# Order of the first FFN group, shared weight buffers, and paced normalizations in a macaron block

## The chip, the cores and the metric

The kernel runs on one core of one Trainium2 chip. The metric is the device time of one execution in microseconds (us); lower is better. The times are medians over runs, and one further execution of each kernel is recorded by the hardware profiler. The engines are named as in the profile: PE is TensorE (matrix products and transposes), DVE VectorE, ACT ScalarE, POOL GpSimd, and SP the engine whose queue issues the loads and stores.

## The reference

The block takes x of 2048 tokens by 512 features, all in float32, and runs an FFN at half weight, a causal attention with 16 heads of 32 features, and the same FFN with the same weights again:

```
x = x + 0.5 * ffn(layernorm(x))
x = x + attention(layernorm(x))
x = x + 0.5 * ffn(layernorm(x))

def ffn(xt):
    gate = einsum('th,nh->tn', xt, Wg)      # 512 -> 4096
    up   = einsum('th,nh->tn', xt, Wu)      # 512 -> 4096
    inter = gelu(gate) * up                 # tanh form
    return einsum('tn,hn->th', inter, Wd)   # 4096 -> 512
```

Wg, Wu and Wd come as 4-bit codes (two in each int32) with one scale for every 32 values, and have to be dequantized.

## The kernel before

**Order.** The program order of an engine's instructions is its order on the chip: the kernel writes out by hand which instruction follows which, and an instruction at the head of an engine's queue that waits holds up what stands behind it. Tiles come from pools; a new tile in a buffer waits until the readers of the old one are done.

**Tokens.** x stays in on-chip memory as 16 tiles of 128 tokens (`xs`), taken as four blocks of 512 (NB) and two pairs of blocks: pair 0 is the early tokens (blocks 0 and 1), pair 1 the late ones (2 and 3).

**Normalization** (`norm_steps`, L79). For a block: moments of each tile on DVE (L88, L89), a square root on ACT for all four tiles (L95) and a reciprocal on DVE (L96). Then, for each tile, the normalized tile xn, on DVE (L107) or with `on_act` on ACT (L105, with a bias from L98), four transposes on PE (L115) and a copy from PSUM on ACT (L116). The steps come as a list: two of statistics (`stats`, two tiles each), then normalize 0, normalize 1, transpose 0, and so on in alternation.

**FFN** (`ffn`, L132). The 4096 hidden features are handled in 8 groups of 512, a group in two row halves: `rows` and `second`, objects of `Rows` (L201) that hold seven weight combinations each for gate and up. In place of eight block products a Strassen-Winograd scheme uses seven, so the weights and the tokens need sums of blocks: the weights' on POOL (L223 to L226), the tokens' by `token_sums` (L238, four operations for a pair of blocks).

A `slot` (L269) is one row half with one pair of blocks: 7 gate products, then 7 up products, each of two 128x512 matmuls in float32 (L264), which the trace records as four matmuls. A product ends in a PSUM bank (a pool of seven) and is evicted on DVE or ACT with additions (L299 to L323); Gelu is on ACT (L282), gate times up on DVE (L286). Behind each product a slot calls `pump(rate)`, which takes `rate` steps from the list `background`, and pops one token sum and one down piece if it has any. The order of products is 1, 2, 6, 7, 5, 4, 3; the first two need no token sum, and the third needs the third sum.

A group is four slots: rows with pair 0, rows with pair 1, second with pair 0, second with pair 1. The 14 down pieces of a token pair (`down_pieces`, L331, matmuls L359) are put into a later slot, those of the last pair behind the last slot, where up to two steps of the next stage's normalization follow each piece from the third on.

**Weights.** In the first FFN they are dequantized on DVE (ten operations per 512 columns of codes, L184 to L192 and L180), and kept in DRAM (L199). The second FFN loads them from there (L210, L457). An FFN has its own two buffers for row halves; the attention has its own buffers for wqk (two pairs of heads at a time), wv, wo and the biases, which it loads at its start, and the second FFN issues its first load when it starts.

**Start of an FFN** (L424 to L455). In the first FFN: normalization of block 0, dequantization of gate, normalization of block 1, the sums of pair 0 on DVE, dequantization of up; then the first slot. Into `background` go the normalizations of blocks 2 and 3, the sums of pair 1 on POOL, and `second`'s dequantization; the first slot runs with rate 4. In the second FFN, blocks 0 and 1 come normalized from the attention's end.

**Attention** (L482). It normalizes blocks 2 and 3 itself, runs over 8 pairs of heads (p) with the projections of later pairs between, divides by the softmax's sums at the end (L687), and closes with the output projection (L572). The projection of heads is `project_qk` (L523), which loads its weights when it is called.

Of the kernel before, what the change touches and what calls it, by code (L numbers as in the profile page):

```python
# [9 lines left out]
F32 = mybir.dt.float32  # L10
F16 = mybir.dt.float16
BF16 = mybir.dt.bfloat16
# [6 lines left out]
P = 128  # L19
S = 2048  # L20
# [14 lines left out]
def macaron_kernel(ctx: ExitStack, tc: tile.TileContext, x, packed, scales, wqk, bqk, wv, bv, wo, bo, out):  # L35
# [16 lines left out]

    xpair = [res.tile([P, 2, D], F32, tag=f"x{t}", name=f"x{t}") for t in range(NT // 2)]
# [11 lines left out]
    nc.gpsimd.memset(eps, EPS)  # L65
    ones_b = const.tile([P, P], BF16, tag="ones_b", name="ones_b")
# [12 lines left out]
    def norm_steps(phase, tb, t_out, temp, on_act=False):  # L79

        nm = f"{phase}_{tb}"
        mv = small.tile([P, 4, 2], F32, tag="mv", name=f"mv_{nm}")
        rstd = small.tile([P, 4], F32, tag="rstd", name=f"rstd_{nm}")
        nbias = small.tile([P, 4], F32, tag="nbias", name=f"nbias_{nm}")

        def moments(i):
            st = small.tile([P, 6], F32, tag="st", name=f"st_{nm}_{i}")
            nc.vector.bn_stats(out=st, in_=xs[4 * tb + i])  # L88
            nc.vector.bn_aggr(out=mv[:, i, :], in_=st)  # L89

        def stats(i):
            moments(i)
            moments(i + 1)
            if i == 2:
                nc.scalar.activation(rstd, mv[:, :, 1], AF.Sqrt, bias=eps)  # L95
                nc.vector.reciprocal(rstd, rstd)  # L96
                if on_act:
                    nc.vector.scalar_tensor_tensor(nbias, mv[:, :, 0], -1.0, rstd, ALU.mult, ALU.mult)  # L98

        xn = [None] * 4  # L100

        def normalize(i):
            xn[i] = temp(f"xn_{nm}_{i}")
            if on_act:
                nc.scalar.activation(xn[i], xs[4 * tb + i], AF.Identity, bias=nbias[:, i : i + 1], scale=rstd[:, i : i + 1])  # L105
            else:
                nc.vector.tensor_scalar(  # L107
                    xn[i], xs[4 * tb + i], mv[:, i, 0:1], rstd[:, i : i + 1], ALU.subtract, ALU.mult
                )

        def transpose(i):
            xnv = xn[i].rearrange("t (jc p b) -> t jc b p", jc=2, b=2)
            pt = ps_one.tile([P, 4, P], F32, tag="one", name=f"pt_{nm}_{i}")
            for k in range(4):
                nc.tensor.transpose(pt[:, k, :], xnv[:, k // 2, k % 2, :], ident)  # L115
            nc.scalar.copy(t_out[:, :, i * P : (i + 1) * P], pt)  # L116

        steps = [lambda i=i: stats(i) for i in (0, 2)]
        for i in range(5):
            if i < 4:  # L120
                steps.append(lambda i=i: normalize(i))
            if i > 0:
                steps.append(lambda i=i: transpose(i - 1))
        return steps

    def x_transposed(phase, tb):
        return res.tile([P, 4, 512], F32, tag=f"xT{tb}", name=f"xT_{phase}_{tb}")
# [4 lines left out]
    def ffn(phase, finish, behind, ready=()):  # L132
# [8 lines left out]
        with tc.tile_pool(name=f"w{phase}", bufs=1) as wp, tc.tile_pool(name=f"dq{phase}", bufs=1) as dq, tc.tile_pool(  # L141
# [59 lines left out]
            class Rows:  # L201
# [3 lines left out]
                def __init__(self, g, h):  # L205
                    self.w = wp.tile([P, 2, 7, 2, P], F32, tag="w", name=f"w_{phase}_{g}_{h}", bufs=2)
                    self.g, self.h = g, h
                    self.codes = [None, None]
                    if phase == 2:
                        nc.sync.dma_start(out=self.w, in_=kept[g, h])  # L210
# [18 lines left out]
                def keep(self):  # L229
                    keep((self.g, self.h), self.w)  # L230
# [38 lines left out]
            def slot(g, rows, tp, sums, fill, rate):  # L269

                b = token_factors(tp)
# [16 lines left out]
                for m, done in ((0, gelu), (1, gated)):  # L288
# [7 lines left out]
                    for i in ORDER:  # L296
# [27 lines left out]
                        pump(rate)  # L324
                        if sums:
                            sums.pop(0)()
# [97 lines left out]
            rows = Rows(0, 0)  # L424
# [6 lines left out]
            for tb in range(NB):  # L431
                xT[tb] = ready[tb] if tb < len(ready) else x_transposed(f"f{phase}", tb)
            norms = [norm_steps(f"f{phase}", tb, xT[tb], normed) if tb >= len(ready) else [] for tb in range(NB)]
            run(norms[0])
            if phase == 1:
                run(rows.steps(0))
            run(norms[1] + token_sums(0, nc.vector))
            if phase == 1:
                run(rows.steps(1))
            background += norms[2] + norms[3] + token_sums(1, nc.gpsimd)  # L440
            fill = ([], [])
            for g in range(NG):
                second = Rows(g, 1)
                if phase == 1:
                    for m in range(2):
                        second.load(m)
                    for m in range(2):
                        background += second.steps(m)
                    rows.keep()
                first = [slot(g, rows, 0, *fill, 2 if g > 0 else 4)]  # L450
                pump(1 << 30)
# [6 lines left out]
                first.append(slot(g, rows, 1, [], [], 1))  # L458
                last = [slot(g, second, 0, [], [], 1)]
# [8 lines left out]
                if phase == 1:  # L468
                    keep(g, wd)
                last.append(slot(g, second, 1, *fill, 2))  # L470
# [3 lines left out]
            steps = behind(normed)  # L474
            for i, piece in enumerate(fill[1]):
                piece()
                if i > 1:
                    run(steps[:2])
                    del steps[:2]
            run(steps)  # L480

    def attention(xT, xT_f):  # L482
        with tc.tile_pool(name="aw", bufs=1) as aw, tc.tile_pool(name="qk", bufs=1) as qkp, tc.tile_pool(
            name="pp", bufs=3
        ) as pp, tc.tile_pool(name="an", bufs=2) as an:
            wqk_sb = aw.tile([P, 2, 4, P], F32, tag="wqk", name="wqk_0")
            nc.sync.dma_start(out=wqk_sb, in_=wqk[0])
            wv_sb = aw.tile([P, 4, D], F32, tag="wv", name="wv_sb")
            bv_sb = aw.tile([P, D], F32, tag="bv", name="bv_sb")
            bqk_sb = aw.tile([P, 2, NQ], F32, tag="bqk", name="bqk_sb")  # L490
            bo_sb = aw.tile([P, D], F32, tag="bo", name="bo_sb")
            wo_sb = aw.tile([P, 4, D], F32, tag="wo", name="wo_sb")
            nc.sync.dma_start(out=bqk_sb, in_=bqk)
            nc.sync.dma_start(out=wv_sb, in_=wv)
            nc.sync.dma_start(out=bv_sb, in_=bv.partition_broadcast(P))
# [6 lines left out]

            mrow = qkp.tile([P, S], BF16, tag="mrow", name="mrow")
# [19 lines left out]
            def project_qk(u):  # L523

                w = wqk_sb
                if u > 0:
                    w = aw.tile([P, 2, 4, P], F32, tag="wqk", name=f"wqk_{u}")
                    nc.sync.dma_start(out=w, in_=wqk[u])

# [268 lines left out]
            }  # L798
            for p in range(NPAIR):
                fills = plan[p]() if p in plan else [[] for _ in range(NB)]  # L800
# [46 lines left out]
    xT_a = []  # L847

    def norms_behind(temp):
        steps = []  # L850
        for tb in range(2):
            xT_a.append(x_transposed("a", tb))
            steps += norm_steps("a", tb, xT_a[tb], temp)
        return steps

    ffn(1, lambda t: None, norms_behind)
    xT_f = []
    attention(xT_a, xT_f)
    ffn(2, lambda t: nc.sync.dma_start(out=out[t * P : (t + 1) * P, :], in_=xs[t]), lambda temp: [], xT_f)
# [64 lines left out]
```

## Time and profile before

| | us |
|---|---|
| runs | 3348.92, 3349.23, 3352.65 |
| median | 3349.23 |
| profiled execution: its time | 3353.61 |
| its span in the trace | 3351.8 |

The mean clock granted to PE over the span is 0.991 of full speed. The page cuts the span into 40 equal slices of 83.8 us. A digit is the busy share in tenths, 9 is 90% or more:

```
PE   5999999999999989999999999899999999999998
DVE  7887777877777555676766784444445455444545
ACT  2111111111111121455543455421111111111111
POOL 2456464644646441322212222122132222313223
PEclk8999999999999999999999999899999999999999
DMA  3111111111111110000000000100110101011101
```

The first FFN takes the first 14 slices, the attention the next 12, the second FFN the rest. PE is busy throughout but in the first slice, in slice 15 (the first FFN's end and the attention's start) and in slice 26 (the attention's end and the second FFN's start). DVE is busier in the first FFN than in the second, which has no dequantization.

Lines of the timeline read: start in us, duration, engine, name of the result where it is one group, line of the kernel, operation, out<-in, shape, count. A bracket gives the idle time of the engine ahead of the line and what ended it.

### The profile page before, as it was taken

The numbers are of one execution on the slowest core, as the hardware profiler recorded it, in microseconds if no ns is written. First come the engines' busy times: TensorE is split into PE (matmuls) and PEld (weight loads), VectorE is DVE, ScalarE is ACT, GpSimd is POOL, SyncE is SP. The second block draws the span as 40 slices with busy tenths as digits, with TensorE's granted clock in tenths as the row PEclk, the third lists the DMA queues.
The fourth block names the chain that finished last, engine by engine and source line by source line (L and its number), as shares of the span: only waits on it lengthen the run. The fifth ranks groups of instructions, "written<-read, shape, count | busy, mean of one in ns | idle before, by whom it ended". The sixth has DMA issues, their size and how long they took to land.

```text
span 3351.8 us, 34007 instructions
## 1 busy us (share of the span) xinstructions
PE 3276.4 (98%) x12640; PEld 1734.2 (52%) x12640; DVE 2128.5 (64%) x3242; ACT 848.4 (25%) x1766; POOL 1157.9 (35%) x1337
## 2 busy tenths in 40 slices
PE   5999999999999989999999999899999999999998
PEld 3556565655656565333344333346565565656556
DVE  7887777877777555676766784444445455444545
ACT  2111111111111121455543455421111111111111
POOL 2456464644646441322212222122132222313223
PEclk8999999999999999999999999899999999999999
DMA  3111111111111110000000000100110101011101
GB/s 104 73 66 66 66 42 68 63 47 68 65 63 48 44 38 7 6 13 6 7 12 4 6 7 7 69 22 22 44 44 28 60 23 44 22 44 44 44 22 51
DMA packets 37941, 132.73 MB, mean 40 GB/s; under 512 B 3984, under 2 KB 20368, under 8 KB 31376
## 3 DMA queue, kind: packets, MB, share of 16 engines
q1 hardware_dynamic: 37776, 130.57, 10.7%
q8 instruction: 99, 1.62, 0.2%
q14 instruction: 66, 0.54, 0.1%
HBM read 78.12 MB, written 48.23 MB: 38 GB/s over the span
## 4 chain that ended last, share of the span: by engine, by line
PE 96%; DVE 3%; ACT 1%; issue 0%; POOL 0%; DMA 0%; SPq 0%; POOLq 0%; ACTq 0%; DVEq 0%
PE po L359 23%; PE pu L264 23%; PE pg L264 23%; PE av L667 8%; PE pm L610 6%; PE pqk L533 4%; PE ps L702 3%; PE ps L711 2%; PE pp L572 2%; PE pv L550 2%; PE pt_f L115 1%; DVE st_f L88 0%; PE pt_a L115 0%; DVE parts L625 0%; PE row L646 0%
## 5 line engine op out<-in xcount | busy, mean ns | idle before, releaser
L264 PE MATMUL pg<-xT_f,w 128*128 128x512 f32 x1024 | 481.6, 599 | 9.4 <-DVE st_f L88 8.0
L359 PE MATMUL po<-wd,inter 128*128 128x256 f32 x2048 | 484.4, 381 | 0.0
L264 PE MATMUL pu<-xT_f,w 128*128 128x512 f32 x1024 | 475.9, 593 | 0.0
L359 PEld LDWEIGHTS po<-wd,inter 128*128 128x128 f32 x2048 | 391.0, 191 | 154.8 <-issue 105.0
L370 POOL TENSOR_TENSOR x<-x,d 128x512 f32<-128x512 f32 x256 | 339.8, 1338 | 352.4 <-DVE d L367 175.7
L316 POOL TENSOR_TENSOR u<-u,u 128x512 f32<-128x512 f32 x128 | 163.2, 1275 | 853.6 <-ACT u L313 845.3
L625 DVE TENSOR_REDUCE parts<-pm 128x1 f32<-128x512 f32 (+3 forms) x640 | 367.3, 604 | 92.9 <-PE pm L610 81.6
L359 PE MATMUL po<-wd,s 128*128 128x256 f32 x1536 | 363.9, 381 | 0.0
L264 PE MATMUL pg<-xsum,w 128*128 128x512 f32 x768 | 356.9, 594 | 0.0
L264 PE MATMUL pu<-xsum,w 128*128 128x512 f32 x768 | 355.4, 593 | 0.0
L359 PEld LDWEIGHTS po<-wd,s 128*128 128x128 f32 x1536 | 293.3, 191 | 116.1 <-issue 79.4
L610 PE MATMUL pm<-kT,qT 32*128 32x512 f32 (+3 forms) x1280 | 338.1, 574 | 0.5 <-DVE parts L625 0.4
L734 ACT ACTIVATE pt<-ps 128x512 f32<-128x512 f32 (+3 forms) x576 | 271.8, 531 | 149.6 <-PE ps L711 148.9
L667 PE MATMUL av<-pt,vaug 128*64 128x512 f32 (+3 forms) x1280 | 304.2, 554 | 0.8 <-ACT both L676 0.6
L264 PEld LDWEIGHTS pg<-xT_f,w 128*128 128x128 f32 x1024 | 196.3, 192 | 205.7 <-issue 188.6
L264 PEld LDWEIGHTS pu<-xT_f,w 128*128 128x128 f32 x1024 | 194.9, 190 | 193.4 <-issue 182.6
L711 PE MATMUL ps<-qT,kT 32*128 32x512 f32 (+3 forms) x1280 | 292.9, 531 | 0.0
L264 PEld LDWEIGHTS pu<-xsum,w 128*128 128x128 f32 x768 | 146.2, 190 | 145.0 <-issue 138.1
L264 PEld LDWEIGHTS pg<-xsum,w 128*128 128x128 f32 x768 | 146.3, 191 | 142.7 <-issue 134.0
L367 DVE SCALAR_TENSOR_TENSOR x<-po,x 128x512 f32<-128x512 f32 x192 | 131.6, 686 | 118.5 <-ACT d L374 85.8
L687 POOL TENSOR_TENSOR attnT<-both,den 32x128 f32<-32x128 f32 x256 | 115.2, 450 | 242.9 <-DVE den L684 174.6
L367 DVE SCALAR_TENSOR_TENSOR d<-po,d 128x512 f32<-128x512 f32 x192 | 131.7, 686 | 84.3 <-PE po L359 82.9
(126 smaller groups left out, 3644.5 us busy)
## 6 DMA issues: line engine op xcount, KB each, us to landing
kept<-wd SPq DMA_DIRECT2D x8, 1792.0 KB
wd<-kept SPq DMA_DIRECT2D x8, 1792.0 KB
x<-in_x SPq DMA_DIRECT2D x16, 256.0 KB
pk<-in_gate_codes SPq DMA_DIRECT2D x16, 256.0 KB
sc<-in_gate_scales SPq DMA_DIRECT2D x32, 128.0 KB
pk<-in_up_codes SPq DMA_DIRECT2D x16, 256.0 KB
sc<-in_up_scales SPq DMA_DIRECT2D x32, 128.0 KB
pk<-in_down_codes SPq DMA_DIRECT2D x16, 256.0 KB
```

The source lines that it names most:

```text
L264: nc.tensor.matmul(ps, lhsT=a[:, j, :], rhs=b[:, j, :], start=(j == 0), stop=(j == 1))
L316: nc.gpsimd.tensor_tensor(u4, u4, u2, ALU.add)
L359: nc.tensor.matmul(ps[:, j, :], lhsT=a[i][:, k, bass.ts(2 * q + j, P)], rhs=b[i][:, k, :], start=(k == 0), stop=(k == 1),)
L367: stt(dst, ps, 0.5, other, ALU.mult, ALU.add)
L370: nc.gpsimd.tensor_tensor(dst, dst, other, ALU.add)
L533: nc.tensor.matmul(ps, lhsT=w[:, j, k, :], rhs=xT[tb][:, k, :], start=(k == 0), stop=(k == 3))
L610: nc.tensor.matmul(ps[a][:, :n], lhsT=q[r, bass.ts(4 * g + i, P)], rhs=k[r, kb * 512 : kb * 512 + n], start=True, stop=not on_pe,)
L625: nc.vector.tensor_reduce(parts[:, a, i, kb : kb + 1], ps[a][:, :n], AX.X, ALU.max)
L667: nc.tensor.matmul(av[64 * a : 64 * a + 64, off:], lhsT=vaug[:, c, p % 4, HD * a : HD * a + 2 * HD], rhs=pt[:, a, off:], start=(c == 0), s ...
L687: nc.gpsimd.tensor_tensor(dst[quadrant(p, a), bass.ts(4 * g + j, P)], both[v, bass.ts(j, P)], rc[v, bass.ts(j, P)], ALU.mult,)
L711: nc.tensor.matmul(ps[a][:, off:], lhsT=k[r, bass.ts(c, P)], rhs=q[r, g * 512 + off : (g + 1) * 512], start=False, stop=True,)
L734: nc.scalar.activation(pt[:, a, plain:], ps[a][:, plain:], AF.Exp, scale=scale)
```

## The change

- **Group 0 of each FFN** has another order of slots: rows with pair 0, second with pair 0, rows with pair 1, second with pair 1. The weights of `second` are dequantized in the first slot (first FFN) or loaded (second FFN). The normalizations of blocks 2 and 3 and the sums of pair 1 leave `background`; they are cut into groups, one behind each product of the second slot. The third slot, with the down weights' dequantization, has rate 2 where before it was 1, and the first slot 2 where it was 4.
- **Normalizations** in an FFN and behind the first one all use `on_act`. `paced` arranges the steps of two blocks in 11 groups: statistics first, then one normalization with the transposes of the tile before.
- **Start of the first FFN**: the steps of the normalizations of blocks 0 and 1 and those of the two dequantizations are interleaved.
- **Sums of pair 1** are on DVE in the second FFN, on POOL as before in the first.
- **Square root**: one on ACT at the program's start, before the first that is needed.
- **Buffers**: one pool of two buffers (`wts`, 14 KB per partition each) for all stages: row halves of both FFNs, wqk + wv + bv, and wo + bo + the attention's bf16 row. So wqk, wv and bv are loaded ahead of the last slot of the first FFN (`load_qkv`), and the second FFN's first row half within the attention, at p == 5 (`load_first`). The loads of wqk for later heads move from `project_qk` to the head of the loop over p.

```diff
+    wts = ctx.enter_context(tc.tile_pool(name="wts", bufs=2))
+    def weights(nm):
+        return wts.tile([P, 7 * 512], F32, tag="w", name=nm)
...
+    nc.scalar.activation(root, eps, AF.Sqrt)
...
+    def paced(first, second):
+        a, b = [s[:2] + [s[2], s[3], s[5], s[7]] + [s[4], s[6], s[8], s[9]] for s in (first, second)]
+        (a0, a1, *a), (b0, b1, *b) = a, b
+        an, at, bn, bt = a[:4], a[4:], b[:4], b[4:]
+        return [
+            [a0], [a1], [b0, an[0]], [b1, an[1], at[0]], [an[2], at[1]], [an[3], at[2]],
+            [bn[0], at[3]], [bn[1], bt[0]], [bn[2], bt[1]], [bn[3], bt[2]], [bt[3]],
+        ]
...
                         pump(rate)
+                        if groups:
+                            run(groups.pop(0))
...
-            run(norms[0])
-            if phase == 1:
-                run(rows.steps(0))
-            run(norms[1] + token_sums(0, nc.vector))
-            if phase == 1:
-                run(rows.steps(1))
-            background += norms[2] + norms[3] + token_sums(1, nc.gpsimd)
+                run(norms[0][:2])
+                gate, up = rows.steps(0), rows.steps(1)
+                run(gate[:4])
+                run(norms[0][2:])
+                run(gate[4:])
+                run(norms[1][:2])
+                run(up[:4])
+                run(norms[1][2:])
+                run(up[4:10])
+                run(token_sums(0, nc.vector))
+                run(up[10:])
...
+            else:
+                run(token_sums(0, nc.vector))
+            last_norms = paced(norms[2], norms[3])
+            sums = token_sums(1, nc.gpsimd if phase == 1 else nc.vector)
+            last_norms[-1].append(sums[0])
+            last_norms += [[s] for s in sums[1:]]
...
-                first = [slot(g, rows, 0, *fill, 2 if g > 0 else 4)]
-                pump(1 << 30)
+                if g == 0:
+                    first = [slot(g, rows, 0, *fill, 2)]
+                    pump(1 << 30)
+                    last = [slot(g, second, 0, [], [], 0, last_norms)]
...
-                first.append(slot(g, rows, 1, [], [], 1))
-                last = [slot(g, second, 0, [], [], 1)]
+                first.append(slot(g, rows, 1, [], [], 1 if g > 0 else 2))
+                if g > 0:
+                    last = [slot(g, second, 0, [], [], 1)]
...
+                if g + 1 == NG:
+                    loads()
...
-            steps = behind(normed)
-            for i, piece in enumerate(fill[1]):
+            groups = behind(normed)
+            for piece in fill[1]:
                 piece()
-                if i > 1:
-                    run(steps[:2])
-                    del steps[:2]
-            run(steps)
+                if groups:
+                    run(groups.pop(0))
+            for group in groups:
+                run(group)
...
+            refill = {1: 2, 3: 3}
+            nc.sync.dma_start(out=wqk_sb, in_=wqk[1])
             for p in range(NPAIR):
+                if p in refill:
+                    nc.sync.dma_start(out=wqk_sb, in_=wqk[refill[p]])
+                if p == 5:
+                    next_w()
```

## Prediction

> **What bounds the kernel now.** I read the page's busy shares and chain first, then busy time by stage, then the order of time at the three places where TensorE (PE) is not busy.
>
> ```profile
> PE 3276.4 (98%) x12640; PEld 1734.2 (52%) x12640; DVE 2128.5 (64%) x3242; ACT 848.4 (25%) x1766; POOL 1157.9 (35%) x1337
> ...
> PE 96%; DVE 3%; ACT 1%; issue 0%; POOL 0%; DMA 0%; SPq 0%; POOLq 0%; ACTq 0%; DVEq 0%
> ```
>
> PE is the bound, and the change leaves its matmuls as they are. So at most the 75.4 us of its idle time (3351.8 - 3276.4) and the stretches at a lowered clock can be won. Stages (columns: length, then busy time of PE, PEld, DVE, ACT, POOL, then clock, DMA share, GB/s):
>
> ```profile
> 0.00:25.70 25.70, 6.94 (x32) 5.88 (x33) 16.60 (x36) 5.67 (x10) 4.93 (x17) 1.00 0.73 224
> 25.70:125.20 99.50, 81.35 (x203) 37.46 (x203) 81.22 (x126) 23.60 (x39) 35.32 (x27) 0.91 0.21 80
> 1184.50:1226.10 41.60, 33.16 (x146) 27.99 (x145) 25.04 (x45) 8.54 (x15) 25.48 (x23) 0.88 0.06 18
> 1226.10:1235.00 8.90, 8.89 (x19) 3.96 (x20) 3.29 (x10) 1.73 (x4) 3.16 (x18) 0.81 0.77 272
> 2151.50:2171.20 19.70, 6.19 (x8) 2.37 (x8) 13.17 (x18) 0.58 (x1) 3.60 (x8) 0.68 0.38 141
> 2171.20:2259.40 88.20, 81.86 (x201) 37.95 (x202) 41.16 (x67) 24.47 (x38) 17.35 (x10) 0.94 0.14 54
> 2259.40:2403.90 144.50, 144.50 (x449) 85.32 (x449) 72.19 (x97) 24.22 (x40) 36.23 (x28) 1.00 0.11 39
> ```
>
> The last row is one steady group of an FFN: no idle PE, full clock. The others are the entry of each FFN and of the attention. How they look in order of time:
>
> ```profile
> 25.76 3.60 PE L264 MATMUL pg<-xT_f,w 128*128 128x512 f32 x8
> 42.18 0.68 DVE L304 TENSOR_TENSOR c<-pg,u 128x512 f32<-128x512 f32 x1
> 43.64 2.98 PE L264 MATMUL pg<-xsum,w 128*128 128x512 f32 x4
> 52.82 3.51 PE L264 MATMUL pg<-xT_f,w 128*128 128x512 f32 x4
> 113.14 12.02 PE pu L264 x28
> ...
> 1195.31 0.74 PE L115 MATMUL pt_a<-ident,xn_a 128*128 128x128 f32 x4 [1.96 <-DVE xn_a L107]
> 1195.89 3.38 PE L359 MATMUL po<-wd,inter 128*128 128x256 f32 x8
> 1226.11 8.80 PE L533 MATMUL pqk<-xT_a,wqk 128*128 128x512 f32 x16 [3.60 <-issue]
> ...
> 2157.05 6.19 PE L572 MATMUL pp<-wo_sb,attnT 128*128 128x512 f32 x8 [5.57 <-POOL attnT L687]
> 2163.28 0.33 SPq L210 DMA_DIRECT2D w<-kept_(0, 0)_300  x1
> 2171.24 5.91 PE L264 MATMUL pg<-xT_f,w 128*128 128x512 f32 x8 [8.00 <-DVE st_f L88]
> 2247.37 12.02 PE pu L264 x28
> ```
>
> To be seen: the first products of an FFN wait until VectorE (DVE) has got through weights, sums and normalizations (its first eviction is at 42.18). The attention waits 3.6 us for its weights, and the second FFN 8.0: DVE's statistics are named there, but the weight load issued at 2163.28 explains the wait better. After such waits 128x512 rows take 0.75 to 0.88 us each (2.98 for 4, 3.51 for 4) where 0.43 is normal (12.02 for 28).
>
> **What the Trainium skill says.** "TensorE: Matmul & The Clock Gate", What's actually happening: PE falls to half clock after an idle window of about 3.4 us and needs about as long to recover, on a free-running window. The trace agrees with half speed for some 3.4 us, but shows it after idle times of only 1.96 and 2.9 us; after 1.14 us there was none. I take 2 us as the point and 1.7 us as the price of a fall. "SBUF — State Buffer", Who interferes with whom: GpSimd (POOL) and DVE lock each other out of a shared port for some operations. The trace agrees: L184 took 1.68 us beside POOL's sums and 0.42 without. "ScalarE: Activation LUTs", What ACT_TABLE_LOAD costs: 1283 ns a load; the trace has 1.28.
>
> **Unit prices**, from the trace: product (2 matmuls) 12.02/7 = 1.72; four transposes 0.47 (8 in 0.95, start to start); down piece 1.73; moments of two tiles 1.6 (L88 + L89); one dequantization on DVE 5.8 (12.11 to 17.94); eviction 0.69; one token sum on DVE 1.25, on POOL 2.4; normalization on ACT 0.82 (L105 in the attention), copy 0.58, Gelu 0.63.
>
> **1. First FFN, up to the end of its third slot** (a slot is 14 products; before: 113.14 + 12.02 = 125.2). The Sqrt table comes ahead of need: 1.28 off the first normalization. Moving xn from DVE to ACT frees 4 x 0.55 per block, and gate's dequantization runs 7.9 to 13.7 while ACT normalizes; block 1's moments end at 16.9, the up dequantization at 23.5, ACT's four normalizations and copies at 23.9, the four sums at 28.9. The first product starts at 23.1; the third needs the third sum, 27.7 (stall 1.2). Then 12 x 1.72: slot one ends at 48.3. DVE has 2 x 5.8 + 16 x 0.69 = 22.6 after 28.9, so 51.5, and I add 1 for the port; the banks (7) cover that lag. Slot two is now the second row half with the late tokens' norms. DVE does moments between evictions; the first rstd waits for a Gelu and a table load, 57.0; xn at 58.3: PE, ready at 55.2, stalls 3.1. ACT then waits in order for the second block's moments (62.0) before the second xn (63.2): about 2 more with the lowered clock. The third xn stands behind a second table load: 1.7. After that ACT's 0.82 + 0.58 + 0.63 per group hide beside 1.72 + 0.47. Seven up products and four transposes more: 84.5. POOL's sums, moved here from slot one, with one u add between, give the needed third sum at 88.5, just after PE's two free products (88.0); slot three ends 12 x 1.72 later, 109.1. The down weights' 24 steps are squeezed into that slot with POOL's sums beside: DVE then has some 28 us in 25; 1 us allowed. End 110: **gain 15** (both ends: 20 if the norm stalls shrink, 8 if DVE's lag breaks the cover and PE waits for evictions).
>
> **2. First FFN to attention.** Last down pieces: with the same 14 pieces and 8 transposes 24.2 + 3.8 are needed from 1184.6. ACT normalizes, one group per piece. Stalls: first transposes wait for xn (1192.2 against 1191.5, 0.8); ACT again stands at the second block's rstd (moments at 1195.2), so the second transposes come at 1196.5 instead of 1194.5: 2.0, and 1.7 for the clock. End 1217.0 against 1222.5: 5.5. Weights loaded in the last group, so no 3.6; pqk at full clock 16 x 0.43 = 6.9 for 8.80: 1.9. Late next: bqk, still issued at the end, but tiny (4 KB) and needed 3.5 us later; the late blocks' xn, whose x sums on POOL end 2.9 us after the last piece as before (2.9 + 1.6 moments + 1.8 on ACT = 6.3, wanted by PE at 6.9). **Gain 11** (7 to 15).
>
> **3. Attention's inside.** PE is full. The wqk loads move a pair of heads earlier, the 1.75 MB FFN load stands in SP's queue ahead of one pair of den copies. Alone such a load took about 8 us (2163.3 to 2171.2); a den copy behind its tail could come some 3 us late, while the reciprocal is taken three steps, about 6.6 us, later. Cost 0, range -1 to 4.
>
> **4. Into the second FFN** (R = 2163.2, end of pp, which stays, with its wait of 5.57). Weights resident: the 8.0 go, and the next wait is the third sum, DVE, at R + 4.4, 1.0 after PE's two free products. Slot one ends at R + 25.1. The second half's load is issued at R and lands in some 8 us, 17 before use. Slot two: stalls 0.7, 2.75 (moments of block 3 end at R + 36.4) and 1.7 for the clock; end R + 58.4. The sums, now on DVE, are done before need (R + 60.5 against 61.8). Slot three ends R + 82.4 = 2245.7, against 2247.37 + 12.02 = 2259.4: **gain 13.7** (9 to 18). The groups after it and the tail are as before.
>
> **Sum.** 15 + 11 + 13.7 = 39.7. The profiled execution took 3353.6 (span 3351.8 and 1.8 around it): 3313.9. The median of the runs is 3349.2, 4.4 below the profiled one; the gain taken from it: 3309.5, so **3310 us**.
>
> **Rivals.**
> - *DVE is the bound in group 0.* For: it is busy 81.2 of 99.5 us there and takes 23 us of work into each 24 us slot. Against: the norms leave it, and 7 banks absorb 12 us. Gain 8 + 7 + 9 = 24: 3325.
> - *The norms' pacing holds better*, stalls under 2 us and no clock falls: 20 + 15 + 18 = 53: 3296. Against: both blocks' moments are early in ACT's order, which I can count out.
> - *The loads are not early after all*, SP standing at a wait ahead of them: 3.6 + 1.9 and 8.0 + 2.5 come back, 16: 3326. Against: the readers that they wait for end a stage before.
> - *Slower.* In slot two each normalized tile waits for the transposes of the one before, since one u3 buffer is left to them. If each of the 8 waits passed 2 us, PE would stand 8 x 2 = 16 us and run the slot at half clock, 24 more; in both FFNs 80, against 39.7 won and 7 of stalls counted already: some 33 slower, 3382. It decides from about 1.2 us of wait per group on. Against: ACT needs about 2.1 us per group, PE 2.2.
>
> **Chances.** Forecast (3300 to 3322) 0.60; DVE bound or loads late 0.18; better pacing 0.12; no change 0.03; slower 0.07. About 0.2% (6.7 us) is what can be told from no change: faster 0.90, same 0.03, slower 0.07. Range 3297 to 3328, which leaves out a little at each end.
>
> **What would show it.** Right: pg from about 23 us, third slot's end near 110; in the down pieces' tail one PE wait of some 2 us on xn; pqk without a wait; pg right behind pp. Wrong: PE waiting for DVE evictions in slots one to three; long rows at 0.85 us all through slot two; a PE gap inside the attention.

## The result, and the profile after

The changed kernel takes 3313.32 us (median of 4 runs, 3312.17 to 3313.88) against 3350.77 for the kernel before in the same series (4 runs, 3348.92 to 3352.65). The ratio is 0.9889, 95% interval 0.9877 to 0.9901: 37.5 us less. The two profiled executions differ by 41.4 (3353.61 and 3312.17). The one of before lies 2.8 above its median, the one of after 1.2 below, and this makes the difference.

Busy shares of the changed kernel, to be set beside the same line of before:

```profile
PE 3265.4 (99%) x12640; PEld 1724.7 (52%) x12640; DVE 2117.7 (64%) x3222; ACT 870.3 (26%) x1798; POOL 1153.2 (35%) x1333
```

PE has the same 12640 matmuls in 11.0 us less busy time (3276.4 before), and its idle time fell from 75.4 to 45.0. So 30 us are waits that went, and 11 are for the most part matmuls that ran at full clock instead of half. The stages of the changed kernel (length, busy time of PE, PEld, DVE, ACT, POOL, clock, DMA share, GB/s), cut at the same events as those of before (to within 0.3 us):

```profile
0.00:22.70 22.70, 8.13 (x32) 6.17 (x33) 17.72 (x40) 11.86 (x19) 4.96 (x17) 1.00 0.82 254
22.70:110.00 87.30, 80.02 (x202) 36.56 (x201) 70.92 (x107) 28.88 (x46) 30.39 (x22) 0.98 0.18 69
1169.80:1200.10 30.30, 28.25 (x144) 24.73 (x144) 15.88 (x33) 14.29 (x23) 20.53 (x17) 1.00 0.00 1
1200.10:1207.00 6.90, 6.90 (x18) 3.01 (x18) 5.30 (x14) 1.80 (x3) 6.84 (x22) 1.00 0.54 191
2123.80:2135.30 11.50, 5.95 (x8) 2.55 (x9) 5.35 (x7) 0.59 (x1) 3.61 (x8) 0.70 0.05 11
2135.30:2217.80 82.50, 77.20 (x201) 35.32 (x200) 48.67 (x76) 28.63 (x45) 7.62 (x6) 1.00 0.12 45
```

Row by row the lengths were 25.7, 99.5, 41.6, 8.9, 19.7 and 88.2 before. The clock column, 0.91, 0.88, 0.81 and 0.94 before in rows two, three, four and six, is at or near 1.00; only the row around the second FFN's start keeps a low one (0.70), since its wait of 5.56 us has stayed. PE's timeline at the same places:

```profile
22.81 4.67 PE L287 MATMUL pg<-xT_f,w 128*128 128x512 f32 x8
28.42 3.67 PE L287 MATMUL pg<-xsum,w 128*128 128x512 f32 x8 [0.94 <-DVE xsum L269]
...
49.09 3.60 PE L287 MATMUL pg<-xT_f,w 128*128 128x512 f32 x8
...
59.39 1.13 PE L127 MATMUL pt_f<-ident,xn_f 128*128 128x128 f32 x4 [3.27 <-ACT xn_f L117]
...
63.93 0.74 PE L127 MATMUL pt_f<-ident,xn_f 128*128 128x128 f32 x4 [0.64 <-ACT xn_f L117]
...
67.53 0.74 PE L127 MATMUL pt_f<-ident,xn_f 128*128 128x128 f32 x4 [1.14 <-ACT xn_f L117]
...
84.49 3.60 PE L287 MATMUL pg<-xT_f,w 128*128 128x512 f32 x8
89.34 3.70 PE L287 MATMUL pg<-xsum,w 128*128 128x512 f32 x8 [1.26 <-POOL xsum L269]
...
110.05 1.88 PE L287 MATMUL pg<-xT_f,w 128*128 128x512 f32 x4
...
1177.27 0.74 PE L127 MATMUL pt_a<-ident,xn_a 128*128 128x128 f32 x4 [0.59 <-ACT xn_a L117]
...
1181.20 0.74 PE L127 MATMUL pt_a<-ident,xn_a 128*128 128x128 f32 x4 [1.46 <-ACT xn_a L117]
...
1200.13 7.03 PE L577 MATMUL pqk<-xT_a,wqk_wv 128*128 128x512 f32 x16
...
2129.36 6.19 PE L616 MATMUL pp<-wo_bo,attnT 128*128 128x512 f32 x8 [5.56 <-POOL attnT L731]
2135.38 3.60 PE L287 MATMUL pg<-xT_f,w 128*128 128x512 f32 x8
2140.02 3.67 PE L287 MATMUL pg<-xsum,w 128*128 128x512 f32 x8 [1.05 <-issue]
...
2168.74 0.74 PE L127 MATMUL pt_f<-ident,xn_f 128*128 128x128 f32 x4 [1.01 <-ACT xn_f L117]
...
2173.26 0.74 PE L127 MATMUL pt_f<-ident,xn_f 128*128 128x128 f32 x4 [2.06 <-ACT xn_f L117]
...
2176.86 0.74 PE L127 MATMUL pt_f<-ident,xn_f 128*128 128x128 f32 x4 [1.14 <-ACT xn_f L117]
```

These are PE's waits of over half a microsecond from the first product to the second FFN's third slot, but for one of 0.57 within the attention. pqk follows the last down piece without a bracket (before: 3.60), and pg follows pp without one (before: 8.00). In both FFNs the second slot waits three times for xn. The lines of DVE and ACT in the first FFN's second slot say why:

```profile
52.86 0.69 DVE L311 TENSOR_TENSOR inter<-u,u 128x512 f32<-128x512 f32 x1
53.47 0.69 DVE L100 BATCH_NORM_STATS2 st_f<-x 128x6 f32<-128x512 f32 x1
...
57.19 0.18 DVE L101 BATCH_NORM_AGGREGATE mv_f<-st_f 128x2 f32<-128x6 f32 x1
...
56.44 1.28 ACT L107 ACT_TABLE_LOAD   x1
57.73 0.30 ACT L107 ACTIVATE rstd_f<-mv_f,eps 128x4 f32<-128x4 f32 x1
58.52 0.81 ACT L117 ACTIVATE xn_f<-x,nbias_f,rstd_f 128x512 f32<-128x512 f32 x1 [0.49 <-ACT rstd_f L107]
...
62.87 0.30 ACT L107 ACTIVATE rstd_f<-mv_f,eps 128x4 f32<-128x4 f32 x1 [3.54 <-DVE mv_f L101]
63.07 0.80 ACT L117 ACTIVATE xn_f<-x,nbias_f,rstd_f 128x512 f32<-128x512 f32 x1
...
64.84 1.28 ACT L307 ACT_TABLE_LOAD   x1
```

The first xn stands behind block 2's root. DVE ends the first slot's work at 53.5, 4.4 us after PE (49.09), begins the moments of block 2 only then and ends them at 57.37; the table load in front of the root ends 0.35 later. In the second FFN, where DVE has no such lag, this wait is 1.01 instead of 3.27. The second xn stands behind block 3's root, for whose moments ACT waits 3.54 us although it has xn to do. The third stands behind the load of Gelu's table.

By the two profiled executions, the time came from: up to the third slot's end of the first FFN 125.00 - 110.05 = 15.0; from there to the attention's first score matmul, 27.76 in all less 15.0, 12.8; within the attention nothing (27.69 at the start of pp); to the third slot's end of the second FFN 41.4 - 27.7 = 13.7 (2259.22 and 2217.86). It stays so to the end (3351.8 and 3310.4). Both kernels are read here at the start of the fourth slot's first product in the timeline; the prediction's 125.2 and 2259.4 come from the view of the chain, which has the same event some 0.2 us later.

### The profile page after: what moved, and what is told of

It is laid out like the page before. It is cut to its first block, busy times and chain, and to the rows that moved or that the text cites. A ratio compares the mean times of both kernels' runs of the same rounds, so it can differ in the third digit from the quotient of the medians.

```text
span 3310.4 us, 34022 instructions
## 1 busy us (share of the span) xinstructions
PE 3265.4 (99%) x12640; PEld 1724.7 (52%) x12640; DVE 2117.7 (64%) x3222; ACT 870.3 (26%) x1798; POOL 1153.2 (35%) x1333
## 4 chain that ended last, share of the span: by engine, by line
PE 95%; DVE 1%; issue 1%; ACT 1%; POOL 1%; DMA 0%; POOLq 0%; SPq 0%; DVEq 0%; ACTq 0%
PE po L386 23%; PE pu L287 23%; PE pg L287 22%; PE av L711 8%; PE pm L654 6%; PE pqk L577 3%; PE ps L746 3%; PE ps L755 2%; PE pp L616 2%; PE pv L594 2%; PE pt_f L127 0%; DVE parts L669 0%; PE pt_a L127 0%; PE row L690 0%; DVE st_f L100 0%
```

## The experiments

Each run edits the changed kernel unless it says otherwise. Three stretches are read from each trace: A, from the span's start to the third slot's end of the first FFN (110.05 in the changed kernel); B, from there to pqk (1090.08); C, from the start of pp to the third slot's end of the second FFN (88.50). A is uncertain by about 1 us: with the same instructions up to the first product, that product starts 19.4 to 20.5 us after the first statistics. The attention, from its first score matmul to pp, takes 913.5 us, but some 915.1 in four of the runs (late loads, old slot order, no preload, one root stage): their traces have one stretch of 3.4 us at half clock within it, the others none. One such stretch costs up to 3.4 / 2 = 1.7 us, and the last section shows that it is partly a matter of chance whether a wait brings one. So a difference of 1 to 2 us in a column below can be one stretch of low clock.

| run | median us | ratio to before (95%) | A | B | C |
|---|---|---|---|---|---|
| changed | 3313.32 | 0.9889 (0.9877-0.9901) | 110.05 | 1090.08 | 88.50 |
| e1 late loads | 3313.06 | 0.9888 (0.9873-0.9903) | +0.4 | 0.0 | -0.2 |
| e1b own buffers | 3326.23 | 0.9934 (0.9919-0.9948) | +0.7 | +3.9 | +9.5 |
| e2 norms on DVE | 3320.44 | 0.9909 (0.9894-0.9924) | +4.6 | +2.2 | -1.2 |
| e3 unpaced | 3329.37 | 0.9937 (0.9921-0.9954) | +8.3 | +1.0 | +7.5 |
| e4 old slot order | 3315.99 | 0.9898 (0.9883-0.9912) | +1.5 | 0.0 | +2.1 |
| e5 plain start | 3318.33 | 0.9908 (0.9893-0.9922) | +5.6 | 0.0 | -0.5 |
| e7 no preload | 3314.82 | 0.9896 (0.9881-0.9911) | +1.9 | 0.0 | -0.2 |
| e6 statistics ahead | 3305.81 | 0.9873 (0.9858-0.9887) | -3.9 | -1.7 | -0.4 |
| e8 products ahead | 3301.35 | 0.9861 (0.9844-0.9877) | -4.7 | -1.7 | -6.9 |
| e9 one root stage | 3298.71 | 0.9847 (0.9830-0.9863) | -4.4 | -1.7 | -8.4 |

The runs were taken in four series: the changed kernel alone; e1, e2, e3 and e4; e1b, e5, e6 and e8; e7 and e9. The median of the kernel before was 3350.77, 3349.61, 3347.97 and 3349.58 in them, so two medians from different series can differ by up to some 3 us without a cause in the kernels.

### The loads: place in the program, or memory?

The first run put the two loads back to where the stages begin:

```diff
-                if g + 1 == NG:
-                    loads()
...
-                if p == 5:
-                    next_w()
...
     ffn(1, lambda t: None, norms_behind, load_qkv)
+    load_qkv()
     attention(xT_a, xT_f, early["qkv"], load_first)
+    load_first()
```

> The changed kernel with its two early loads put back: wqk, wv and bv are loaded when the first FFN has ended, the first row half when the attention has ended; buffers, order and normalizations stay. My theory: the two waits come back where they were, pqk some 3.6 us and its first 16 rows at 8.8 instead of 6.9 (5.5 in all), and pg behind pp some 8 us with about 2.4 for the lowered clock, 10 in all: 15 to 16 over the changed kernel's 3313, 3329. Rival: the 8.0 before pg belonged to the DVE statistics that the trace of before named; then pg waits under 1.5 us and the kernel takes about 3319.

It took 3313.06 us and no wait came back: neither theory foresaw that. SP's queue in that run shows that the loads were not late on the chip:

```profile
1116.52 0.39 SPq L909 DMA_DIRECT2D wqk_wv<-in_wqk  x1
...
2127.59 0.57 SPq L915 DMA_DIRECT2D w<-kept_(0, 0)_306  x1
```

wqk is issued at 1116.5, as in the changed kernel (1116.1), since nothing that waits stands ahead of it in SP's queue. The row half is issued at 2127.6 instead of 1835, behind the last copies of the softmax sums, still 9.5 us ahead of its use at 2137.1. So this run could not tell the cause of the waits. It showed that a later place in the program costs nothing here: wqk's issue did not move, and the row half's, though 293 us later, was early enough. The next run left order and normalizations as changed and gave each stage buffers in its own pools again, with the loads where the stage starts, as in the run with late loads; so the memory is what sets these two runs apart:

```diff
-    wts = ctx.enter_context(tc.tile_pool(name="wts", bufs=2))
...
-                    self.flat = weights(...) if w is None else w
+                    self.flat = wp.tile([P, 7 * 512], F32, tag="w", ..., bufs=2)
...
+            wqk_wv = aw.tile([P, 7 * 512], F32, tag="wqk_wv", name="wqk_wv")
+            wo_bo = aw.tile([P, 7 * 512], F32, tag="wo_bo", name="wo_bo")
```

> The changed kernel with each stage's weights in buffers of that stage's own pools again, as before, loaded when the stage starts; order and normalizations stay as changed. In the run with late loads the queue had issued them early all the same, so place in the program was not what counted. My theory now: what holds a load back is memory that lies under the tiles of the stage before; with own buffers pqk waits some 3.6 us (5.5 with the clock) and pg behind pp about 8 (10 with the clock): 3326 to 3331. Rival: the waits had another cause (DVE's statistics at pg, the transposes at pqk), which the new order has removed: 3311 to 3317.

SP and PE of this run, in order of time:

```profile
1201.03 0.33 SPq L534 DMA_DIRECT2D wqk_wv<-in_wqk  x1
1204.71 10.03 PE L575 MATMUL pqk<-xT_a,wqk_wv 128*128 128x512 f32 x16 [3.72 <-issue]
...
2143.37 0.33 SPq L229 DMA_DIRECT2D w<-kept_(0, 0)_303  x1
2151.18 6.11 PE L283 MATMUL pg<-xT_f,w 128*128 128x512 f32 x8 [7.84 <-issue]
```

The loads are issued when the last matmul of the stage before has ended, and both waits are back with their lowered clock: 10.03 for 16 rows against 7.03, 6.11 for 8 against 3.60. It costs 12.9 us (3326.23 - 3313.32). The stretches of the traces agree (3.9 in B and 9.5 in C). So the shared buffers are worth about 13 of the 37.5, and the DVE statistics which the trace of before named at pg were not the cause of that wait.

### Normalizations on ACT

```diff
-                norm_steps(f"f{phase}", tb, xT[tb], normed, True) if tb >= len(ready) else [] for tb in range(NB)
+                norm_steps(f"f{phase}", tb, xT[tb], normed) if tb >= len(ready) else [] for tb in range(NB)
...
-        return paced(*[norm_steps("a", tb, xT_a[tb], temp, True) for tb in range(2)])
+        return paced(*[norm_steps("a", tb, xT_a[tb], temp) for tb in range(2)])
```

> The changed kernel with the FFN's normalizations, and those behind the first FFN, back on DVE, in the same order and pacing. My theory: DVE is what the start waits for, so eight tiles of 0.55 us there cost some 4 us at the third sum of the first slot (third slot's end 114 to 116 for 110.05), and the tail 1 to 3; the second FFN loses nothing, since DVE has room there, and may win 1 to 2 of ACT's waits. 3317 to 3321. Rival: DVE has slack and ACT's order is what costs; then the time is 3313 or less.

3320.44 us, 7.1 more, and spread as expected: 4.6 at the start, where DVE's third sum comes late (PE waits 3.48 us for it instead of 0.94), 2.2 in the tail, and 1.2 less in the second FFN. That rival is out; ACT's order does cost, but only where DVE has room.

### Pacing

```diff
     def paced(first, second):
-        a, b = ...
+        steps = first + second
+        return [steps[i : i + 2] for i in range(0, len(steps), 2)]
```

> The changed kernel with the groups of normalization steps as plain pairs in the old order (two statistics, two normalizations, then a transpose with each further one, first block first). My theory: PE reaches the first transposes one product earlier and those of the second block two products after their statistics, so both blocks cost a wait of 3 to 5 us in each FFN's second slot where the changed kernel has one of 3.3 and small ones: 2.5 to 4 more in each FFN and about 2 in the down pieces' tail, 3319 to 3323. Rival: the pacing costs rather than brings, since both blocks' statistics stand early in ACT's order (0.6 to 2 us there); then 3309 to 3313.

3329.37 us, 16 more: the direction of the theory with twice its size, in A and C. PE's waits in the second slot:

```profile
60.97 1.13 PE L127 MATMUL pt_f<-ident,xn_f 128*128 128x128 f32 x4 [5.67 <-ACT xn_f L117]
...
69.70 0.74 PE L127 MATMUL pt_f<-ident,xn_f 128*128 128x128 f32 x4 [0.95 <-ACT xn_f L117]
...
79.13 0.74 PE L127 MATMUL pt_f<-ident,xn_f 128*128 128x128 f32 x4 [3.53 <-ACT xn_f L117]
...
86.85 0.74 PE L127 MATMUL pt_f<-ident,xn_f 128*128 128x128 f32 x4 [0.95 <-ACT xn_f L117]
```

11.1 us of waits where the changed kernel has 5.1, and 10.2 us of half clock in A where it has 3.4. The second block, whose statistics come two products before its first transposes, pays 3.53 again. With the statistics of both blocks in front, ACT stands at the second root once, and the second block has no wait at all.

### Order of the slots

The paced normalizations are run in the first slot, and the second slot is again rows with pair 1, with `second`'s dequantization:

```diff
-                    background += second.steps(m)
...
-                    first = [slot(g, rows, 0, *fill, 2)]
+                    first = [slot(g, rows, 0, *fill, 0, last_norms)]
+                    if phase == 1:
+                        for m in range(2):
+                            background += second.steps(m)
+                    first.append(slot(g, rows, 1, [], [], 2))
                     pump(1 << 30)
-                    last = [slot(g, second, 0, [], [], 0, last_norms)]
...
+                last = [slot(g, second, 0, [], [], 1 if g > 0 else 2)]
```

> The changed kernel with group 0's old order of slots (rows early, rows late, second early), the paced normalizations in the first slot and the second half's dequantization in the second slot. My theory: the gain at the start of the first FFN comes from the interleaved start and the norms on ACT, and the order of slots only says which work DVE does first; 3310 to 3318, third slot's end 108 to 114. Rival: the order itself brings it, since late tokens are needed a slot later; then the third slot ends at 118 or later and the kernel takes 3321 or more.

3315.99 us: 2.7 more, with the third slot's end at 111.6: the theory's side. The order is worth little, and not shown to be worth anything: in A and in C this trace has one stretch of 3.4 us more at half clock, up to 1.7 us each, which is about what it loses there (1.5 and 2.1). The work of DVE is the same in either, and only changes places: the waits for xn move into the first slot (3.68 and 1.05), and POOL's third sum is late by the same 1.26.

### The start of the first FFN, and the Sqrt table

```diff
-                run(norms[0][:2])
-                gate, up = rows.steps(0), rows.steps(1)
-                ...
+                run(norms[0])
+                run(rows.steps(0))
+                run(norms[1] + token_sums(0, nc.vector))
+                run(rows.steps(1))
```

> The changed kernel with the start of the first FFN in the old sequence (normalization of block 0, gate, normalization of block 1, sums, up), normalizations still on ACT. My theory: DVE then waits some 6 us for the last transposed tile before its sums, with the up dequantization behind them, so that the up products or the second slot's statistics come 4 to 6 us late: 3317 to 3320, all of it before the third slot's end. Rival: with ACT doing the normalizations the sequence no longer matters: 3312 to 3314.

3318.33 us, 5.0 more, all in A. DVE's timeline of this run has the idle time, and PE's the place where it is paid:

```profile
17.33 0.16 DVE L110 SCALAR_TENSOR_TENSOR nbias_f<-mv_f,rstd_f 128x4 f32<-128x4 f32 x1
23.93 1.23 DVE L267 TENSOR_TENSOR xsum<-xT_f 128x1024 f32<-128x1024 f32 x1 [6.43 <-ACT xT_f L128]
...
64.97 1.13 PE L127 MATMUL pt_f<-ident,xn_f 128*128 128x128 f32 x4 [9.30 <-ACT xn_f L117]
```

DVE stands 6.43 us at the first sum, with the up dequantization queued behind it. The first slot doesn't notice (it even ends 0.4 earlier); the debt falls due at the second slot's statistics, 9.30 instead of 3.27.

The early square root was removed alone:

```diff
-    nc.scalar.activation(root, eps, AF.Sqrt)
```

> The changed kernel without the early square root, so that the Sqrt table is loaded when the first root is needed. My theory: the load of 1.28 us stands in the chain from the first statistics to the first normalized tile and nothing hides it; DVE, which waits for the root, carries it on: first product and third slot's end 1.3 later, 3314 to 3316. Rival: DVE's lag in the first two slots is absorbed by the banks, so that it is gone by the third slot's end: 3312 to 3313.5.

3314.82 us, 1.5 more, A 1.9 later. This agrees with 1.3, but the range of A in kernels with the same start is about 1, so it is not shown apart from the rival.

### Removing what is left

The waits for xn should go if the first root is ready before the second slot and the second doesn't stand before the first block's xn. The statistics of block 2 go into the first slot, those of block 3 to products two and three of the second; DVE gets the room by taking part of the up dequantization into the second slot, and xn lies in the down sums' tile, which is not yet in use:

```diff
+        return [[]] * 7 + [[a0], [a1], [], [], [ar], [], [an[0]]], [
+            [an[1], at[0]], [b0, an[2], at[1]], [b1, an[3], at[2]], [at[3]], [br], [bn[0]],
+            [bn[1], bt[0]], [bn[2], bt[1]], [bn[3], bt[2]], [bt[3]],
+        ]
```

> The changed kernel with the statistics of block 2 and its first normalization in the first slot, those of block 3 spread over products two and three of the second slot and its root behind the fifth, half of the second row half's up dequantization moved into the second slot to make room on DVE, the normalized tiles in memory of their own, and in the tail the second block's root one group later. My theory of the waits (first root too late, then ACT standing at the second root and at a table load): 7.4 us in the first FFN, 5.2 in the second and 1.5 in the tail go, and at most 4 come back by ACT's load: 3299 to 3306. Rival: DVE, behind by 4 us at the end of the first slot, is the real bound, and PE then waits for its evictions or for POOL's weights instead: 3311 or more.

3305.81 us, 7.5 less and at the upper edge of the expectation. The early waits and POOL's 1.26 are gone, but one wait of 3.16 (first FFN) and one of 2.93 (second) have appeared at block 3's first xn, now behind its root and two table loads. In the second FFN this wait and a stretch of half clock behind it take nearly all back (C -0.4). B's 1.7 is the tail, where the wait of 1.46 is gone, since the second root comes one group later there.

The next kernel adds to it work for PE in the wait before pp: the second FFN's first two products, whose weights are resident, and three of its token sums on DVE, ahead of the divisions. The sums lie in a tile kept for both FFNs.

```diff
+            sub_(t[:, 0], b22, b12)
+            sub_(b12, b12, b11)
+            sub_(t[:, 1], b22, b12)
             for step in divisions:
                 if step:
                     step()
+            sub_(t[:, 2], b21, t[:, 1])
+            for i, (a, b) in enumerate(((w0[:, 0, 0], b11), (w0[:, 0, 2], b21))):
+                ps = ps_one.tile([P, 512], F32, tag="one", name=f"pg{i + 1}_2_0_0_0")
+                early_ps.append(ps)
+                for j in range(2):
+                    nc.tensor.matmul(ps, lhsT=a[:, j, :], rhs=b[:, j, :], start=(j == 0), stop=(j == 1))
             for piece in o3[12:]:
                 piece()
```

> The kernel with the statistics ahead, and also the second FFN's first two products and three of its four token sums ahead of the attention's last output projections, where PE waits 5.57 us for the divisions. My theory: 3.4 us of products fill that wait and the rest, about 2.1, is too short to lower the clock, so pp takes 3.5 for 6.0 to 6.2, and the wait of 1.05 for the third sum goes: 5 to 7 less than the kernel with the statistics ahead. Rival: the sums delay the reciprocals by 1.5 us or more and the clock falls all the same: 1 to 3 less.

3301.35 us, 4.5 less; by C, 6.5 less, of which up to 1.7 is chance: the wait of 2.93, which this kernel has too, brought no half clock in this execution. POOL and DVE have their lines beside PE's:

```profile
2117.41 3.70 PE L936 MATMUL pg<-xT_f,w 128*128 128x512 f32 x8
...
2123.19 5.74 PE L643 MATMUL pp<-wo_bo,attnT 128*128 128x512 f32 x8 [2.08 <-POOL attnT L758]
2124.24 1.50 POOL L758 TENSOR_TENSOR attnT<-both,den 32x128 f32<-32x128 f32 x1
2124.28 1.16 DVE L923 TENSOR_TENSOR xsum<-xT_f,xsum 128x1024 f32<-128x1024 f32 x1
2128.76 3.60 PE L301 MATMUL pg<-xsum,w 128*128 128x512 f32 x8
```

The wait shrank from 5.56 to 2.08, and the third product follows pp at once. The rival's late reciprocals did not come: pp starts 929.54 us after pqk, against 929.35 with the statistics ahead. The term that failed is pp: 5.74 us, not 3.5. The clock did fall after the 2.08, but at full clock pp would not have taken 3.5 either: POOL's eight products took 5.1 us, its fifth 1.50 beside DVE's fourth sum where the others took 0.45, and PE began the sixth of pp's eight matmuls 4.13 us after the first, when POOL had ended its last.

The last kernel puts the statistics of both blocks into the first slot and both roots one after the other, with the up dequantization wholly in the second slot:

```diff
+        return [[]] * 6 + [[a0], [a1], [b0], [b1], [], [ar], [], [an[0]]], [
+            [an[1], br, at[0]], [an[2], at[1]], [an[3], at[2]], [at[3]], [], [bn[0]],
+            [bn[1], bt[0]], [bn[2], bt[1]], [bn[3], bt[2]], [bt[3]],
+        ]
```

> The kernel with the products ahead, and the statistics of both late blocks in the first slot, both roots one after the other, so that the Sqrt table is loaded once and no root stands between the gate's Gelus; the second half's up dequantization wholly in the second slot. In the kernel with the products ahead one wait of 3.16 us (first FFN) and one of 2.93 (second FFN) is left, behind the second root and two table loads. My theory: both waits go, with 0 to 1.5 of clock: 5 to 7 less, 3294 to 3297. Rival: DVE, with 1.3 us more in the first slot, is late with the weights for the up products or at the first Gelu of the second slot, and gives back 2 or more in the first FFN: 3298 or more.

3298.71 us, which is the rival's side: 2.6 less than the kernel with the products ahead, from another series, and the intervals of the two ratios overlap, so this step is not shown to be clear of noise. By the traces it gains 1.5 in C and loses 0.3 in A. In the first FFN the wait of 3.16 has become 0.43, but DVE is late at the second slot's first Gelu and a new one of 2.28 stands there. By the median this version is the fastest of the study, 14.6 us below the changed kernel.

## Why the prediction was right

It forecast 3310 and 39.7 us of gain; the traces have 41.4, the medians 37.5. The mechanism was right in its main lines. The time is 3.3 too low because the gain was read from a trace whose execution was slower than the median, and taken from the median. In other series the slower executions of the kernel before have the lower mean clock (last section), so a part of that gain is probably clock falls that a median execution doesn't have. The prediction's own 3313.9, the profiled execution less the gain, is 0.6 off.

| step | predicted gain | trace | decided by |
|---|---|---|---|
| 1, first FFN's start | 15 | 15.0 | e2, e3, e4, e5, e7 |
| 2, to the attention | 11 | 12.8 | e1, e1b, e2 |
| 3, attention's inside | 0 | 0.1 less | trace alone |
| 4, second FFN's start | 13.7 | 13.7 | e1b, e2, e3 |

**Step 1** holds in its parts: slot one's end at 48.3 was 49.09, slot two's at 84.5 was 84.49, the third sum at 88.5 was 89.34, the third slot's end at 110 was 110.05. The stall at the first xn, 3.1, was 3.27; that at the second was put at about 2 with the clock and was 0.64 and about 1.5 of slow matmuls; the third, 1.7, was 1.14. That the end is met to 0.05 is luck: the terms of the second slot, added up from the second xn at 63.2, give 83.7 and not 84.5, the third sum came 0.8 late, and the microsecond allowed for DVE's lag in the third slot was not needed, since PE waited for no eviction. What the prediction did not split, the runs did: normalizations on ACT 4.6, the interleaved start 5.6, the order of the slots at most 1.5, and plain pairs in place of the pacing would cost 8.3. These overlap, have their share of clock falls in them, and aren't to be added.

**Step 2** was 1.8 too low, mainly by one term: the 1.7 charged to the tail for a fall of the clock. PE waited 0.59 and 1.46 there, where 0.8 and 2.0 were expected, and ran at full clock; against that, the pieces and transposes took 28.5 and not 28.0. The weight wait went as said, but for another reason than the step gives: "Weights loaded in the last group" is what the program says, and the run with late loads shows that this place was not needed; the memory is what counts. The rival of loads that come late rested on SP standing at a wait; that didn't happen. Its price, put at 16, was 12.9 in the run with own buffers.

**Step 3** held; PE shows no new gap. Since no run moved the refills of wqk alone, this rests on the comparison of the traces.

**Step 4**: the wait for the third sum, 1.0, was 1.05; the stalls of slot two, 0.7 and 2.75, were 1.01 and 2.06, with a third of 1.14 that the step did not name, and no clock fall in place of the 1.7. These errors nearly cancel: the end of slot two, R + 58.4, came 58.45 us after the first product's start behind pp. The missing fall is in part luck of this execution, as the last section shows.

**Rivals.** DVE as the bound of group 0 is refuted in its own form (no wait for an eviction), but not altogether: at the start DVE is what everything waits for, as the runs with normalizations on DVE and with the plain start show, and its lag from the first slot makes most of the wait of 3.27 in the second (1.01 in the second FFN). Slower by a chain through one u3 buffer is refuted: no wait follows the third tile, and the kernel with separate memory for xn shows its one wait of over half a microsecond in that slot at a root and its table loads. Better pacing was met half-way: no clock falls in the tail and in the second FFN's slots, but three waits remain in each FFN, the longest 3.27 and 2.06 us.

## What to carry to other kernels

A load at the start of a stage waits for memory as much as for its place in the program: look when the queue issued it, and if that is when the last matmul of the stage before ended, give it a buffer that outlives stages, not an earlier line. A wait that an engine pays late can stem from an idle stretch of another engine 40 us before, so follow the debt back (DVE's 6.4 us at the first sum, paid at the second slot's statistics). On an engine that works in order, put what waits for others (here the second root) behind what is ready, and count the table loads that each switch of function adds. Before two traces are compared over some microseconds, count the stretches of half clock in each.

## What the runs showed of the hardware

The length of a wait does not decide by itself whether PE's clock falls after it; its place in time does, too. The Trainium skill, "TensorE: Matmul & The Clock Gate", What's actually happening, gives a window of 3413 ns that runs freely; the prediction took 2 us of wait as a point, from the trace of before. The traces agree with the free window: in each of the twelve, all switches of the granted clock lie on one grid of 3.4133 us, to within 3 ns, and the grid starts at another point in every execution. It cuts waits. The kernels with the statistics ahead and with the products ahead have the same wait of 2.93 us in the second FFN's second slot. In the views of stages, cut at the grid (columns as above; the clock is the third number from the end), the first two lines are of the one kernel and the last three of the other:

```profile
2169.12:2172.53 3.41, 0.48 (x3) 0.26 (x3) 1.54 (x4) 3.37 (x6) 0.00 (x0) 1.00 0.00 0
2172.53:2175.94 3.41, 3.41 (x8) 1.79 (x8) 0.00 (x0) 1.40 (x3) 0.00 (x0) 0.50 0.00 0
...
2161.76:2165.17 3.41, 2.11 (x5) 0.57 (x3) 1.08 (x5) 3.26 (x4) 0.70 (x1) 1.00 0.00 0
2165.17:2168.58 3.41, 1.78 (x7) 1.16 (x8) 0.54 (x1) 3.26 (x6) 0.00 (x0) 1.00 0.00 0
2168.58:2171.99 3.41, 3.41 (x15) 2.09 (x14) 0.43 (x1) 2.53 (x5) 0.00 (x0) 1.00 0.00 0
```

In the one, the whole wait lies in a single window, and the next window runs at half clock. In the other it is cut into 1.30 and 1.63, and the clock stays. It is the same with the waits of 1.96 (before) and 2.08 (products ahead), which lie in one window and were followed by half clock, and that of 2.06 (changed), which is cut into 0.75 and 1.32 and was not. Over all twelve traces, a window at full clock with more than 2.0 us without PE work was always followed by one at half clock; between 1.89 and 2.00 there were two of each kind; below, none but the four in the attention, where PE was idle for only 0.7 us of the window and whose cause stays open. So the skill's idle window need not be idle throughout: some 2 us of it were enough here.

From this a chance can be estimated. If a wait lies anywhere on the grid and 1.95 us in one window are needed, a wait of 2.06 us brings a fall in about 45% of executions and one of 2.93 us in about 70%. So the prediction's 1.7 us for a wait of that length is better priced with such a share. It is likely also why executions of one kernel differ: in one series, those of the kernel before ran from 3346.59 us at a mean clock of 0.994 to 3355.2 us at 0.989.

SP's queue ran 84 us ahead of PE: in the run with late loads the load that the program has after the whole first FFN was issued at 1116.5, and PE came to its products at 1200.5.
